# A two-layer attention and correlation network on one core: a planner's durations, the places it waits for, and when loads and token sums are queued

## The chip, the cores and the metric

The kernel runs on one core of a Trainium2 chip. The time is the device time of one execution in microseconds (us); three executions of the kernel before took 2810.83, 2817.05 and 2821.6 us, and the median, 2817.05, is the figure to which the change is compared. A separate, profiled execution took 2814.8 us, and all views below are of that one.

The engines named here: TensorE (PE in the profile; PEld is its weight load), VectorE (DVE), ScalarE (ACT), GpSimd (POOL) and SyncE (SP), whose queue issues nearly all DMAs.

## What is computed

Eight images of 768 channels and 32 x 32 = 1024 tokens pass two layers, each added to its input. All is f32.

```python
# layer 0
x_flat = gn(x) as tokens                       # 1024 x 768
q, k, v = x_flat @ W_qkv.T, 12 heads of 64
var_v, var_k = var(v, -1, ddof=1), var(k, -1, ddof=1)
attn = softmax(var_v @ var_k.T * scale)        # outer product of two vectors, per head
x = x + (attn @ v) @ W_proj.T + b_proj
# layer 1
f = gn(x)
n = f / max(norm(f over channels), 1e-12)
corr = [sum over channels of shifted(n) * n, for 28 shifts of a 7 x 7 window]
x = x + conv_w @ concat(f, corr) + conv_b
```

The scores of a head are an outer product of two vectors of 1024 numbers, so a block of exponentials needs only one row (broadcast to 128 partitions) and one column.

## The kernel before

*Products.* The large products are done by a seven-product scheme on 2 x 2 blocks (a form of Strassen's): a unit is one of the seven products p of one output group. Keys and values take 28 units of each half of the heads for an image (three matmuls of 384 columns each, two instructions a matmul); the projection and the convolution take 21 units each (three of 512 columns). Sums of weight blocks are made once at the start and kept in DRAM; sums of token blocks are made for each image, for keys and values by GpSimd (line 520, `make_sums`) and for the two wide products by VectorE (`TokenSums`, lines 931 to 967: `first` makes t1, `second` t2, `thirds` overwrites a part of f, `fourth` makes t4; three VectorE instructions each). Products p = 6 read t2, p = 7 the thirds, p = 4 t4.

*Weight blocks.* `KvStream` (line 267) keeps five buffers of 576 KB for key and value blocks, each of which serves two units; `TStream` (line 288) keeps seven of 192 KB for the wide products, one for each unit. After a unit's matmuls are queued, `done` (line 283) or `Wide.unit` (line 892, its last line) queues the refill of the freed buffer on SP at once.

*Attention.* The twelve heads are six pairs; pairs 0 to 2 need the first half of keys and values, 3 to 5 the second. A pair has eight steps t. A step makes two tiles of exponentials on ScalarE (line 651, from a broadcast row `bc` that a DMA reads back from DRAM, `vdr`), and four matmuls (line 676), two instructions each, add to one PSUM tile `av`. TensorE takes four steps in a row, a run of 32 instructions. There are six buffers of exponentials, three steps' worth (AHEAD). The denominators come in one of two ways: on ScalarE, by a second pass of exponentials with an accumulated sum (line 661, from the row `bk`, read back from `kdr`), or, for the pairs in SUMMED (3 to 5; in image 0 all but pair 1), by VectorE, which adds the tiles of exponentials into two `acc` tiles, two additions of 128 x 1024 a step; a buffer of such a pair is free when both its products and its addition are done. After the last step the pair's `av` is copied by ScalarE (`evacuate`, line 696), the sums are made into inverses, by way of DRAM (`di`, `den`, `rd`) or, for the last pair, from PSUM by VectorE, and `finish` multiplies.

*Second layer.* It runs one image behind: while image b has its attention, image b - 1 has its Gram products (line 974, eight of them) and its convolution (`Conv`, line 1063), whose residual, image b - 1 after layer 0, is read back from DRAM into the freed image buffer. `Corr` turns the Gram products into 28 correlations; matmuls of these with their weights join two convolution units at a time (line 905).

*The order.* Nothing is scheduled by the compiler. The program is emitted once, in Python, and an engine executes its instructions in the order in which they were emitted; the semaphores keep them right. That order is decided by a planner (`Clock`, line 71), which passes a planned time `now` on as units are queued on TensorE: `KV_US`, `T_US`, `CORR_US` and `STEP_US` are what it takes a unit, a joined correlation and a step to be, and 2.5 us for a Gram product. `later.after(us, job)` emits a job when the planned time has come that far. ScalarE has a planned time of its own, `act`: two rows of work wait for it, the exponentials (each 2 x EXP) and ScalarE's sums (each SUM); `feed_act` (line 92) emits the next when `act` is at most 1 us ahead of `now`, and of both rows takes the exponentials, unless these are ready over 0.3 us later. `clock.dve` is VectorE's planned time (line 126).

`exp_work` (line 835) says when a step's exponentials may be made: when the pair's rows are taken to be there (`rows_at`, line 644: 6 us after they are asked for) and fewer than AHEAD steps are made and not yet multiplied. `can_run` (line 865) lets a run of four steps begin when three steps are made and the last of them is due within 1 us. In `work_off` (line 1139) a run goes ahead of the remaining units, and while the attention is not over, units worth TAIL = 14 us are kept back for its end.

```python
841            def may():
842                if ("c", 1) not in pair.rows_at or self.made - self.done >= AHEAD or self.made - self.summed > LAG:
843                    return None
844                return max(pair.rows_at["c", 1], clock.now if self.made - self.done == AHEAD - 1 else 0.0)
...
875            return self.made >= self.done + AHEAD and self.exp_at <= clock.now + 1.0
```

After attention and convolution comes the projection (`project`, line 1156), four units of which need no more than pairs 0 to 2; the fifth waits for the last pair's result. Its residual, the image, is loaded into the buffer of f.

In image 0 there is no second layer to fill with, and the loads of the correlation weights (`load_corr_weights`, line 396, due at planned time 150), 29 of them with the copy to the second half of the partitions, fall into its attention.

Of the kernel before, what the change touches and what calls it, by code (L numbers as in the profile page):

```python
# [18 lines left out]
HP = NH // 2  # L19
MT = N // P  # L20
# [21 lines left out]
AHEAD, LAG = 3, 4  # L42
# [2 lines left out]
TBLOCKS = 7  # L45
HELD = 12
TAIL = 14.0
EXP, SUM, STEP_US = 1.08, 1.28, 1.92
KV_US, T_US, CORR_US = 1.95, 2.58, 0.9

# [99 lines left out]
def two_layers(ctx, tc, x, wkv, wproj, bproj, wconv, wcorr, bconv, out):  # L152
    nc = tc.nc
# [5 lines left out]
    xnpool = pool("xnpool", 1)  # L159
# [22 lines left out]
    clock = Clock()  # L182
    later = clock
# [16 lines left out]
    def image_tile(pl, tag, name):  # L200
        return pl.tile([P, J, N], F32, tag=tag, name=name)

    def load(t, src, *queues):
        for j in range(J):
            (queues or (nc.sync,))[j % max(len(queues), 1)].dma_start(out=t[:, j, :], in_=src[:, j, :])
        return t
# [60 lines left out]
    class KvStream:  # L267
# [13 lines left out]
                self.loaded += 1  # L281

        def done(self, key):
            self.gone.add(key)
            del self.tiles[key]
            self.fill()

    class TStream:
        def __init__(self):
# [61 lines left out]
    xn = load(image_tile(xnpool, "xn", "xn0"), xv[0], nc.sync, nc.scalar)  # L351
    sums0 = WeightSums(0, nc.sync, nc.scalar)
    kv_stream, t_stream = KvStream(), TStream()
# [4 lines left out]
    for base, sign in ((0, 1), (3, -1)):  # L358
        nc.gpsimd.affine_select(
            out=group, in_=group, compare_op=ALU.is_ge, fill=0.0, base=base,  # L360
# [262 lines left out]
    class Pair:  # L623
# [13 lines left out]
        def rows(self, kind, e):  # L637

            pl, of = (bcpool, self.kv.vdr) if kind == "c" else (bkpool, self.kv.kdr)
            h = self.heads()[e][1]  # L640
            bc = pl.tile([P, N], F32, tag=f"b{kind}", name=f"b{kind}{self.b}_{self.hp}_{e}")
            nc.sync.dma_start(out=bc, in_=windows(of[self.half][h : h + 1, :], (0, P), (1, N)))
            (self.bc if kind == "c" else self.bk).append(bc)
            self.rows_at[kind, e] = clock.now + 6.0

        def exponentials(self, t):

# [155 lines left out]
    class Attention:  # L803


        def __init__(self, b, kv, ots):
            self.b, self.kv = b, kv
            self.pairs = []
            for hp in range(HP):
                self.pairs.append(Pair(b, hp, kv, ots[hp], self.pairs[-1] if hp else None))  # L810
            self.made = self.done = self.summed = 0
            clock.poll = self.load_rows
            for pair in self.pairs:
                for t in range(MT):
                    self.exp_work(pair, t)
                for e in range(2):
                    for t in range(MT):
                        self.sum_work(pair, t, e)
# [16 lines left out]
        def exp_work(self, pair, t):  # L835
            def may():
                if ("c", 1) not in pair.rows_at or self.made - self.done >= AHEAD or self.made - self.summed > LAG:
                    return None
                return max(pair.rows_at["c", 1], clock.now if self.made - self.done == AHEAD - 1 else 0.0)

            def job():
                pair.exponentials(t)
                self.made += 1
                self.exp_at = clock.act

            clock.act_work(2 * EXP, may, job)
# [30 lines left out]
        def run(self):  # L877
            hp, t0 = divmod(self.done, MT)
            for t in range(t0, t0 + STEPS):
                while t not in self.pairs[hp].exs:  # L880
                    clock.pass_time(0.25)
                self.pairs[hp].products(t)
                self.done += 1
                clock.pass_time(STEP_US)


    class Wide:
# [4 lines left out]
        def unit(self, g, p):  # L892
            w = t_stream.take(self.kind, g, p)
            pairs = [(w[:, k, :], self.operand(p, k)) for k in range(JH)]
            taken = lambda ps: self.take(g, p, ps)
            more = self.more(g, p) if self.more else None
            if more is None:
                banks.product(g, p, T_US, HF, pairs, taken)
            else:
                self.held.append((*banks.begin(g, p, HF, pairs, stop=False), taken, *more))  # L900
                if len(self.held) == 2:
                    self.join()
            t_stream.fill()

        def join(self):

# [156 lines left out]
    class Conv:  # L1063
# [7 lines left out]

        def start(self):
            if self.acc is None:
                self.acc = load(image_tile(xnpool, "xn", f"x1_{self.b}"), x1_dram[self.b])
            if self.b == NB - 1:
                self.sums.third = [expool.tile([P, N], F32, tag="ex", name=f"t3_{k}")[:, :HF] for k in range(JH)]
            self.sums.second()
            self.wide = Wide(
                "c", f"c{self.b}", self.acc, bconv_sb, self.sums.operand, lambda i, hf: self.done(i, hf, "f"), self.more
            )  # L1080
            ready.add(("acc", self.b))
            later.after(4.0, self.thirds)

        def more(self, g, p):

# [51 lines left out]
    x1_dram = {}  # L1137
# [94 lines left out]
    for b in range(NB + 1):  # L1232
        rest, attention, ots = [], None, None
        if b < NB:

            ots = [v.rearrange("p t r d -> p (t r d)") for v in kv.vt]
            rest += kv.units(1)
            attention = Attention(b, kv, ots)
        if b:
            clock.wait(("f", b - 1), ready=ready)  # L1240
            f, acc = layer1[b - 1]
            corr = Corr(b - 1, f)
            conv = Conv(
                b - 1, f, None if b < NB else acc, (lambda b=b: next_image(b + 1)) if b + 1 < NB else lambda: None
            )
            grams = [(2.5, (), lambda t=t: corr.gram(t)) for t in range(MT)]
            first, start = (0.0, (), conv.sums.first), (0.0, (), conv.start)
            if b < NB:
                for n, gram in enumerate(grams):
                    rest.insert(3 * (n + 1) + n, gram)  # L1250
                rest.insert(len(rest) - 4, first)
                rest += [start] + conv.units()
            else:
                units, parts = conv.units(), conv.corr_units()
                rest += [first, start] + units[:2] + grams + units[2:17] + parts[:1] + units[17:19] + parts[1:] + units[19:]
        elif NB > 1:
            rest.insert(len(rest) - 1, (0.0, (), lambda: later.after(24.0, lambda: load_image(1))))
        work_off(rest, attention)
        if b == 0 and NB > 1:
            later.after(24.0, lambda: first_norm(1, images[1], 1.0))  # L1260
        if b < NB:
            project(b, ots)
            if b + 1 < NB:
                clock.wait(("xn", b + 1), ready=ready)
                kv = KeysValues(b + 1, images[b + 1])
                work_off(kv.units(0))
            else:
                clock.wait(("f", b), ready=ready)
# [36 lines left out]
```

## Time and profile before

| | us |
|---|---|
| median of three executions | 2817.05 |
| profiled execution | 2814.8 |
| its span, first to last instruction | 2812.8 |
| granted TensorE clock, share of full | 0.992 |
| one image of images 1 to 6, from pair 0's first run to the next one's (1083.36 to 1423.52) | 340.2 |
| exponentials, line 651: 768, mean 1.139 each | 833.5 busy |
| ScalarE's sums, line 661: 352, mean 1.144 each, and 0.187 to read the sum out | 402.6 and 66.0 busy |
| VectorE's sums `acc<-acc,ex`: 364, mean 1.216 each | 419.3 busy |
| attention products, line 676: 3072, mean 0.605 each | 735.2 busy |
| DMA engines, mean busy share of 16 | 50.8% |

The span is the time between the first and the last instruction; about 2 us of the execution lie outside it. A mean of one instruction counts from its own start to its own end; instructions of one engine overlap, so the distance from start to start is shorter: four exponentials in a row take 4.25 us. Matmuls are drawn with ends that are modelled, two of them at a time on different columns for line 676, and a busy TensorE can be one that waits within a group: a group is measured from its start to the start of what comes next.

### The profile page before, as it was taken

What the parts mean: (1) busy time and instruction counts of PE and PEld (TensorE: products, weight loads), DVE (VectorE), ACT (ScalarE), POOL (GpSimd) and SP (SyncE); (2) the same over time, 40 slices, a digit from 0 to 9 for tenths busy, and PEclk for the clock granted to TensorE, in tenths of its full rate; (3) what the DMA queues carried; (4) which work ended last, traced back from release to release, by engine and by line L of the source; (5) the groups of instructions that cost most, each with busy time, mean ns of one, the idle gap of its engine ahead of it and who ended that gap; (6) DMA issues with size and microseconds to landing.
All of it is one profiled execution on the core that took longest, in us unless ns stands there. A gap on an engine that the chain in (4) does not pass through costs nothing.

```text
span 2812.8 us, 28872 instructions
## 1 busy us (share of the span) xinstructions
PE 2737.1 (97%) x9070; PEld 1287.5 (46%) x9070; DVE 1627.1 (58%) x4086; ACT 1365.5 (49%) x1875; POOL 310.9 (11%) x350
## 2 busy tenths in 40 slices
PE   6988999999999999999999999999999999999999
PEld 3432455335553355534554345543455334553354
DVE  4778733776337753477534875258642676437753
ACT  1466039820597106970088701985019840298300
POOL 3500120002200022000310002100121001210000
PEclk9999999999999999999999999999999999999999
DMA  8573354545554555536456265453654626535323
GB/s 298 195 255 113 124 170 132 177 134 192 174 146 140 181 160 168 161 118 204 152 161 188 85 210 166 149 173 94 225 183 114 190 77 229 167 107 165 111 83 95
DMA packets 320923, 447.67 MB, mean 159 GB/s; under 512 B 59862, under 2 KB 242870, under 8 KB 320770
## 3 DMA queue, kind: packets, MB, share of 16 engines
q1 hardware_dynamic: 318962, 440.70, 50.0%
q10 hardware_dynamic: 1808, 5.11, 0.5%
q8 instruction: 73, 1.20, 0.2%
q14 instruction: 80, 0.66, 0.1%
HBM read 377.83 MB, written 65.81 MB: 158 GB/s over the span
## 4 chain that ended last, share of the span: by engine, by line
PE 82%; DMA 9%; ACT 4%; DVE 2%; SPq 2%; issue 1%; POOL 0%; DVEq 0%; ACTq 0%; POOLq 0%
PE x L338 32%; PE av L676 19%; PE y L338 14%; PE z L338 9%; PE gr L979 4%; ACT ex L651 4%; DMA bc<-vdr 1%; DMA kv<-kvs 1%; DMA vdr<-rsv 1%; DMA bk<-kdr 1%; DMA kdr<-rsk 1%; DMA wt<-tsc 1%; DVE acc L146 1%; DMA v<-rows 1%; DMA f<-in_x_dram 1%
## 5 line engine op out<-in xcount | busy, mean ns | idle before, releaser
L651 ACT ACTIVATE ex<-bc,nk 128x1024 f32<-128x1024 f32 x768 | 833.5, 1139 | 363.8 <-DMA bc<-vdr 243.4
L676 PE MATMUL av<-ex,v 128*64 128x512 f32 x3072 | 735.2, 605 | 29.1 <-ACT v L209 15.2
L676 PEld LDWEIGHTS av<-ex,v 128*64 128x64 f32 x3072 | 229.6, 138 | 512.6 <-issue 366.4
L146 DVE TENSOR_TENSOR acc<-acc,ex 128x1024 f32<-128x1024 f32 x364 | 419.3, 1216 | 2.2 <-ACT ex L651 2.2
L661 ACT ACTIVATE junk<-bk,vm 128x1024 bf16<-128x1024 f32 x352 | 402.6, 1144 | 31.0 <-DMA bk<-kdr 25.4
L209 ACT COPY kp<-x 128x384 f32<-128x384 f32 x32 | 15.2, 479 | 716.8 <-PE x L338 716.8
L338 PE MATMUL y<-kv,s 128*128 128x384 f32 x768 | 267.0, 488 | 2.7 <-DMA kv<-kvs 2.7
L338 PE MATMUL x<-kv,s 128*128 128x384 f32 x768 | 262.5, 490 | 3.8 <-DMA kv<-kvs 3.8
L338 PE MATMUL x<-kv,xn 128*128 128x384 f32 x768 | 262.0, 490 | 3.8 <-DVE xn L146 3.3
L338 PEld LDWEIGHTS x<-kv,s 128*128 128x128 f32 x768 | 145.4, 191 | 111.5 <-issue 13.8
L338 PEld LDWEIGHTS x<-kv,xn 128*128 128x128 f32 x768 | 145.4, 191 | 108.5 <-issue 10.4
L338 PEld LDWEIGHTS y<-kv,s 128*128 128x128 f32 x768 | 143.5, 190 | 96.5 <-POOL s L525 3.3
L146 DVE TENSOR_TENSOR v<-y,v 128x128 f32<-128x128 f32 x192 | 43.8, 283 | 197.7 <-PE y L338 197.7
L979 PE MATMUL gr<-f 128*128 128x227 f32 (+1 forms) x672 | 131.2, 345 | 0.0
L338 PE MATMUL x<-v,wt 128*128 128x512 f32 x288 | 130.1, 597 | 0.0
L338 PE MATMUL z<-kv,xn 128*128 128x384 f32 x384 | 129.2, 486 | 0.0
L979 PEld LDWEIGHTS gr<-f 128*128 128x128 f32 x672 | 121.3, 191 | 13.5 <-issue 1.5
L446 POOL TENSOR_TENSOR rstda<-vea,neghalf 128x1 f32<-128x1 f32 x8 | 4.8, 596 | 1046.1 <-DVE vea L146 1046.1
L525 POOL TENSOR_TENSOR s<-xn 128x384 f32<-128x384 f32 x64 | 67.4, 1057 | 465.7 <-PE x L338 362.8
L338 PE MATMUL x<-f,wt 128*128 128x512 f32 x252 | 117.2, 601 | 0.0
L146 DVE BATCH_NORM_STATS2 kbn<-x 128x6 f32<-128x64 f32 x384 | 56.4, 215 | 91.8 <-PE x L338 91.8
L146 DVE BATCH_NORM_STATS2 vbn<-v 128x6 f32<-128x64 f32 x768 | 108.4, 210 | 0.0
(163 smaller groups left out, 2856.4 us busy)
## 6 DMA issues: line engine op xcount, KB each, us to landing
kv<-kvs SPq DMA_DIRECT2D x128, 576.0 KB
kv<-in_wkv_dram SPq DMA_DIRECT2D x96, 576.0 KB
bc<-vdr SPq DMA_DIRECT2D x96, 512.0 KB
f<-in_x_dram SPq DMA_DIRECT2D x48, 512.0 KB
xn<-in_x_dram SPq DMA_DIRECT2D x45, 512.0 KB
bk<-kdr SPq DMA_DIRECT2D x44, 512.0 KB
x1d<-f SPq DMA_DIRECT2D x42, 512.0 KB
x<-x1d SPq DMA_DIRECT2D x42, 512.0 KB
```

The lines of the kernel that those rows point to most:

```text
L146: return getattr(self.engine, name)(*args, **kw)
L209: nc.scalar.copy(to, at)
L338: nc.tensor.matmul(t, lhsT=lhsT, rhs=rhs, start=p in FIRST and k == 0, stop=stop and k == len(pairs) - 1, skip_group_check=True,)
L446: nc.gpsimd.tensor_tensor(self.rstd, ve, neghalf[:, 0:1], ALU.pow)
L525: nc.gpsimd.tensor_tensor(self.sums[g][:, 0], a[g][2], a[g][3], ALU.add)
L651: nc.scalar.activation(ex, self.bc[e], AF.Exp, scale=self.kv.nk[self.half][:, h, t : t + 1])
L661: nc.scalar.activation(junk, self.bk[e], AF.Exp, scale=self.kv.m2[self.half][:, h, t : t + 1], accum_out=self.sums[:, e, t : t + 1],)
L676: nc.tensor.matmul(self.av[e * HD : (e + 1) * HD, hf, :], lhsT=self.vt[:, t, e, :], rhs=exs[e][:, hf * HF : (hf + 1) * HF], start=t == 0, ...
L979: nc.tensor.matmul(ps[:, :n], lhsT=f[:, j, t * P : (t + 1) * P], rhs=f[:, j, t * P : t * P + n], start=j == 0, stop=j == J - 1,)
```

## The change

It alters numbers and the time of emission. No instruction of an engine is added or taken away, apart from the residual's six loads being written out one by one as before they were in a loop.

- The planner's durations: EXP 1.08 to 1.07, SUM 1.28 to 1.15, STEP_US 1.92 to 1.77, KV_US 1.95 to 1.94, T_US 2.58 to 2.6, CORR_US 0.9 to 1.05; a Gram product 2.5 to 2.35, the last and narrower one to 1.45.
- A key and value block's buffer counts as free, and its refill is queued, KV_US + 0.3 after the unit; a wide block's refill T_US + 0.3 after its unit.
- The rows of pairs 0 and 3 are taken to be there 9 us after they are asked for.
- `may` now takes as the time from which a step's exponentials can be made the end of the products of the step whose buffers it takes over, and for VectorE's pairs also the end of its sums, less one exponential. This is noted in `free_at` as each step is queued.
- The residual's six chunks are loaded in the order 0, 1, 3, 4, 2, 5, at 0, 1, 2.5, 4, 12 and 14 us after the convolution's start; `second` goes 3.5 us after the start instead of at it, `thirds` (and `fourth` behind it) 7 instead of 4.

```diff
-EXP, SUM, STEP_US = 1.08, 1.28, 1.92
-KV_US, T_US, CORR_US = 1.95, 2.58, 0.9
+EXP, SUM, STEP_US = 1.07, 1.15, 1.77
+KV_US, T_US, CORR_US = 1.94, 2.6, 1.05
...
         def done(self, key):
-            self.gone.add(key)
             del self.tiles[key]
-            self.fill()
+
+            def free():
+                self.gone.add(key)
+                self.fill()
+
+            later.after(KV_US + 0.3, free)
...
-            self.rows_at[kind, e] = clock.now + 6.0
+            self.rows_at[kind, e] = clock.now + (9.0 if self.hp % (HP // 2) == 0 else 6.0)
...
             self.made = self.done = self.summed = 0
+            self.free_at = []
...
-                return max(pair.rows_at["c", 1], clock.now if self.made - self.done == AHEAD - 1 else 0.0)
+                free = self.free_at[self.made - AHEAD] if self.made >= AHEAD else 0.0
+                return max(pair.rows_at["c", 1], free)
...
-                self.pairs[hp].products(t)
+                pair = self.pairs[hp]
+                pair.products(t)
+                self.free_at.append(max(clock.now + STEP_US, clock.dve - EXP if pair.summed else 0.0))
                 self.done += 1
...
-            t_stream.fill()
+            later.after(T_US + 0.3, t_stream.fill)
...
             if self.acc is None:
-                self.acc = load(image_tile(xnpool, "xn", f"x1_{self.b}"), x1_dram[self.b])
+                self.acc = image_tile(xnpool, "xn", f"x1_{self.b}")
+                for n, us in ((0, 0.0), (1, 1.0), (3, 2.5), (4, 4.0), (2, 12.0), (5, 14.0)):
+                    later.after(us, lambda n=n: nc.sync.dma_start(out=self.acc[:, n, :], in_=x1_dram[self.b][:, n, :]))
...
-            self.sums.second()
+            later.after(3.5, self.sums.second)
...
-            later.after(4.0, self.thirds)
+            later.after(7.0, self.thirds)
...
-            grams = [(2.5, (), lambda t=t: corr.gram(t)) for t in range(MT)]
+            grams = [(2.35 if t < MT - 1 else 1.45, (), lambda t=t: corr.gram(t)) for t in range(MT)]
```

## The prediction

> **What bounds the kernel now.** I read the page first, then the waits of TensorE, its timeline through one whole image, the chain of waits through the same stretch, and last the queue of SyncE (SP).
>
> The page's first part, busy time by engine:
> ```profile
> PE 2737.1 (97%) x9070; PEld 1287.5 (46%) x9070; DVE 1627.1 (58%) x4086; ACT 1365.5 (49%) x1875; POOL 310.9 (11%) x350
> ```
> TensorE is busy nearly throughout, so no other engine can be worth much unless it makes TensorE stand. Who does that, in total us, times and longest:
> ```profile
> PE av L676 <- ACT v L209: 15.2, 5, 4.1
> PE pma L431 <- DVE mva L146: 14.1, 1, 14.1
> PE av L676 <- ACT ex L651: 12.8, 16, 4.4
> PE x L338 <- DVE t2o L146: 8.0, 3, 6.9
> ```
> Start and image 0 hold most of that. But a busy matmul may be a waiting one, so I go by start times. TensorE's timeline in image 4 (the fifth): start, duration, group, and in brackets idle time before it:
> ```profile
> 1423.52 5.37 PE L676 MATMUL av<-ex,v 128*64 128x512 f32 x24
> 1429.17 2.97 PE L676 MATMUL av<-ex,v 128*64 128x512 f32 x8 [0.29 <-ACT ex L651]
> ...
> 1540.32 7.24 PE L676 MATMUL av<-ex,v 128*64 128x512 f32 x24
> 1547.80 2.97 PE L676 MATMUL av<-ex,v 128*64 128x512 f32 x8 [0.24 <-ACT ex L651]
> 1550.70 0.28 PE L785 MATMUL it<-ident,inv 128*16 128x128 f32 x1
> ...
> 1554.54 7.09 PE L676 MATMUL av<-ex,v 128*64 128x512 f32 x32
> 1561.56 2.84 PE L338 MATMUL x<-f,wt 128*128 128x512 f32 x6
> ```
> An undisturbed run of four steps takes 7.02 from start to start (1554.54 to 1561.56). The run at 1540.32, the first of pair 3, takes 10.38: 3.36 lost. The one at 1423.52, the first of pair 0, takes 8.55 (the next product starts at 1432.07): 1.53 lost. Counted this way over images 1 to 7: pair 0's first run loses 1.90, 1.65, 1.73, 1.53, 1.56, 4.66, 4.78 (17.8 in all); pair 3's 2.99, 2.88, 3.50, 3.36, 3.29, 3.43, 2.06 (21.5); the last pair's two runs (14.04 undisturbed) 1.52, 1.33, 1.29, 1.24, 1.51, 2.89, 2.01 (11.8). Together 51. The rest of an image runs without gaps. Image 0, which has no second layer to fill with, loses some 47 more: 172.71 to 204.25 holds 72 products worth 15.8 in 31.55, the three pair borders after it lose about 17, t2o 8.7 at 273 to 292, and the runs at 110.56 and before 126.52 another 5.
>
> The chain of waits at pair 3 of the same image, start and duration:
> ```profile
> 1522.25 8.86 DMA v<-rows
> 1535.24 4.95 DMA bc<-vdr
> 1541.33 4.25 ACT ex L651 x4
> ```
> and SP's timeline there and in image 0:
> ```profile
> 170.81 0.33 SPq L789 DMA_DIRECT2D di<-ir  x1
> ...
> 182.58 0.46 SPq L498 DMA_DIRECT2D vdr<-rsv  x1
> 183.08 1.13 SPq L748 DMA_DIRECT2D rd<-di  x2
> ...
> 1516.92 4.02 SPq L205 DMA_DIRECT2D x<-x1d  x6
> ...
> 1532.53 0.53 SPq L498 DMA_DIRECT2D vdr<-rsv  x1
> 1534.86 2.02 SPq L642 DMA_DIRECT2D bc<-vdr  x4
> ```
> VectorE had the row for vdr ready at 1527.8 (its copy starts at 1527.55, 0.28); it left at 1532.53. In image 0, 29 small loads of the correlation weights sit between 171.2 and 182.5, ahead of vdr and rd. What SP itself waits for:
> ```profile
> SPq L279 <- PE x L338: 428.7, 104, 14.6
> SPq L302 <- PE x L338: 301.8, 123, 10.7
> ```
> These are refills of weight buffers, queued before the product that frees the buffer has run; everything behind them waits too.
>
> [...] 24 products drawn as 7.24 need 24 x 0.219 = 5.27. [...] so a refill that waits holds the queue; the 428.7 above is that. [...] the trace's mean is 1.216, its start-to-start 1.145 (9.16 for eight). [...]
>
> **The change part by part.** No product, exponential or byte is added: 384 attention steps and 224 + 336 weight blocks stay. All edits move instructions within their engines' orders, through a planner's clock.
>
> *Durations.* A step was planned at 1.92 and takes 1.755; it becomes 1.77. Two exponentials and two sums of ScalarE were 2 x 1.08 + 2 x 1.28 = 4.72, become 4.44, and take 4.50 in the trace (1457.00 to 1461.53, 1461.53 to 1466.03). A Gram product goes from 2.5 to 2.35, takes 2.29; a joined correlation from 0.9 to 1.05, takes 1.06. Engine against engine little moves, since both sides were planned 6 to 9% long: by this alone about nothing. ScalarE is now planned 1.3% short: over the 24 steps of pairs 0 to 2, 1.4 us, a bit more where sums follow sums (1.28 against 1.15). The bound is 0 to +2 an image; I take +1, 8 with small shifts elsewhere.
>
> *Rows at +9 instead of +6 for pairs 0 and 3.* The planner releases a run when the third step's exponentials are due within 1 us: 6 + 3 x 2.16 - 1 = 11.5 after the rows are asked for, now 9 + 6.42 - 1 = 14.4. TensorE takes one more product (1.94 or 2.6) first; there are 28 and 21 to draw on, so it costs nothing there. Lost today: 1.5 to 3.5, and 4.7 in images 6 and 7. Of pair 0's 17.8 I take 15 (3 stay in images 6 and 7, where 4.7 exceeds the 2.9). Of pair 3's 21.5 I take 20, since vdr also leaves earlier, as follows.
>
> *Weight refills later* (1.94 + 0.3 and 2.6 + 0.3 after their product's issue). 219 and 329 DMAs reach SP about when their buffer is free, so they are issued about when they are now, but other DMAs pass them. Cover: a kv block serves two products, four other blocks 15.5 us, landing in about 5; a wt block has six units, 15.5, landing in up to 9.1 (the chain at 2204.42). A further 2.9 still fits. If the cover were gone, each late block would cost its excess, 0 to 2; I take 0.
>
> *Residual loads and token sums.* Six loads of 512 KB leave at 0, 1, 2.5, 4, 12, 14 instead of as one 4.02 us burst on SP, in order of need; the three token sums (1.88 each for three) go 3.5 later. Passed by: spread's nine small operations (about 1.9), vdr, bc. t2 has ten us of products before its use, at t2 +3.5 + 1.9; thirds and fourth are needed five units later still. Cost 0 (bounds -1 to +2, VectorE waiting at the first residual chunk 1.84 as now). vdr gains up to 4.7; included above.
>
> *Places freed by sums.* In summed pairs the planner now has a place free when VectorE's sum ends. Its next run is due later by about a unit where VectorE lags, which fills TensorE where it waits in the last runs: 5 of 11.8. Evacuation of a pair's result is planned at 1.97 after the last product, and one exponential step fewer stands ahead of it: in image 0, where ScalarE did two steps (224.60 x2 among them) between the end of the products and the copies, 2.1 at up to three pair boundaries: 4 of 6.3. There too, the shorter plan puts the 29 loads (due at planned 150) some 3 us of work later: with even chance behind vdr and rd, 8.6 saved or none: 4.
>
> Sum: -15 - 20 - 5 - 8 + 8 = -40. From the profiled execution's own 2814.8 (span 2812.8) that is 2774.8; its run lies 2.25 under the median of 2817.05: 2777.
>
> **Rivals.**
> *The waits move on* (0.22). The later runs meet a ScalarE that has started its own chain later; pair 0's wait for its bk rows (2.80 before a sum at 1426.84) stands ahead of the fourth step all the same. For it: these gaps end in a DMA. Against: 2.9 us more cover is larger than most gaps. Then only a quarter of 51 goes: 2817 - 12 = 2805.
> *Image 0 gives its whole due* (0.10): 8.6 + 6.3 + 3 at 126.52, and last runs fully: another 20, 2757.
> *Attention ends too late* (0.18). VectorE's sums are planned at 1.215 each against 1.145, and every run of pairs 3 to 5 may be put off by a unit: 6 x 2.58 = 15.5, and 6 from the rows. Behind the last run lie 26.4 us of second-layer units (1608.65 to 1635.09); the planner keeps 14 back, so 12.4 can be spent. Beyond, TensorE waits: 21.5 - 12.4 = 9.1 in each of seven images, 64, less the 42 of first runs and image 0 that stay: 2839. It decides from about 18 us of delay an image. Against it: at a pair's border both planners wait for the same denominators, so only three runs move: about 8.
>
> **How the numbers follow.** 0.50 for the main case, 2760 to 2800. Measurement tells about 0.5%, 14 us: faster is under 2803. Faster: 0.50 + 0.10 + 0.06 of the first rival = 0.66. Same: 0.16 + 0.02 of the last = 0.18. Slower 0.16. Range 2752 to 2826: it takes in the first rival and the shallow part of the last, and leaves out some 0.04 below, 0.12 above.
>
> **What would show it.** Runs of pair 0 and 3 at 7.1 from start to start; L279 and L302 waits on SP cut to a third; vdr issued within a microsecond of its row; x<-x1d no longer in one piece; fewer than eight units behind the last run. Wrong would be: those runs whole, but new gaps at x<-t2o or at the last pair (the last rival), or kv and wt among what TensorE waits for.

## The result and the profile after

The changed kernel takes 2890.72 us (median of four executions, 2885.1 to 2893.15) against 2815.65 for the kernel before on the same chip. The ratio is 1.0263 [1.0237, 1.0289]: slower by 75 us, where 40 less had been forecast. The profiled execution took 2892.71, its span is 2891.0 (before 2812.8), its granted clock 0.980 (before 0.992). "Loss" means from here on, as in the prediction, the time from a group's start to the start of what follows, less that of an undisturbed group.

The page's first part hardly shows it:

```profile
PE 2749.9 (95%) x9070; PEld 1286.9 (45%) x9070; DVE 1644.4 (57%) x4086; ACT 1359.9 (47%) x1875; POOL 311.3 (11%) x350
```

The same number of instructions, 95% instead of 97% of a longer span. What TensorE waits for does show it (line, releaser; total us, times, longest):

```profile
PE x L917 <- DMA cs<-cs: 29.1, 7, 5.0
PE x L342 <- DMA wt<-tsp: 24.0, 6, 6.1
PE av L680 <- ACT ex L655: 19.9, 12, 8.4
...
PE ct L1033 <- DVE dn L146: 10.2, 7, 1.5
```

The first two are new. Each comes about once an image, and both are DMAs. TensorE's timeline of image 4 (start, duration, group, in brackets the idle time before it) has pair 0's first run, pair 3's, and the two waits:

```profile
1468.66 5.37 PE L680 MATMUL av<-ex,v 128*64 128x512 f32 x24
1475.04 2.97 PE L680 MATMUL av<-ex,v 128*64 128x512 f32 x8 [1.01 <-ACT ex L655]
1477.94 2.57 PE L987 MATMUL gr<-f 128*128 128x227 f32 x12
...
1587.66 1.12 PE L917 MATMUL y<-cs,wcorr_sb 64*128 64x512 f32 x2
1593.07 2.07 PE L917 MATMUL x<-cs,wcorr_sb 64*128 64x512 f32 x2 [4.29 <-DMA cs<-cs]
1595.07 8.97 PE L680 MATMUL av<-ex,v 128*64 128x512 f32 x32
1603.97 2.84 PE L342 MATMUL x<-f,wt 128*128 128x512 f32 x6
...
1701.65 2.74 PE L342 MATMUL x<-v,wt 128*128 128x512 f32 x6
1708.39 4.38 PE L342 MATMUL x<-v,wt 128*128 128x512 f32 x6 [4.00 <-DMA wt<-tsp]
1712.61 2.74 PE L342 MATMUL y<-v,wt 128*128 128x512 f32 x6
```

Pair 0's run loses 2.26 (9.28 from 1468.66 to 1477.94, less 7.02), more than the 1.53 of before. Pair 3's loses 1.88 instead of 3.36. Ahead of that run now stand the first joined correlations, which before came behind it, and wait for `cs`. The group after each wait is long too: six matmuls at 1708.39 take 4.22 to the next group, where such a group elsewhere takes 2.6. The clock by stretches around the wait for `cs` (us of the stretch, PE busy, granted clock, DMA share, GB/s):

```profile
1588.00:1592.00 4.00, 0.78 (x2) 1.00 1.05 292
1592.00:1595.00 3.00, 1.93 (x2) 0.51 0.89 221
1595.00:1604.00 9.00, 9.00 (x34) 0.78 0.16 60
1604.00:1611.00 7.00, 7.00 (x23) 1.00 0.22 58
```

Four idle microseconds are followed by a stretch at half clock, and most of it falls into the run. So a wait costs more than its length: 1.6 us more at 1708.39 (4.22 instead of 2.6, with a clock of 0.66 from 1708 to 1713), and 2.8 more at 1593.07 (0.9 in the two joined products, 1.9 in the run). Over the whole span the lower clock accounts for at most (1 - 0.980) x 2891.0 = 58 us, before for at most (1 - 0.992) x 2812.8 = 23; at most, because part of the half clock falls into the waits themselves (1592.1 to 1593.07 of the one for `cs`).

The chain of waits, start and duration, names what each waited for:

```profile
1582.58 10.45 DMA cs<-cs
...
1687.94 8.81 DMA out_dram<-x
...
1699.79 8.46 DMA wt<-tsp
```

and SP's timeline says why these were late:

```profile
1579.27 1.77 SPq L646 DMA_DIRECT2D bc<-vdr  x4
1581.09 1.45 SPq L1084 DMA_DIRECT2D x<-x1d  x2
1582.58 0.82 SPq L1066 DMA_DIRECT2D cs<-cs  x1
...
1688.41 0.52 SPq L306 DMA_DIRECT2D wt<-tsp  x1
1696.83 2.92 SPq L205 DMA_DIRECT2D xn<-in_x_dram  x6
1699.79 1.26 SPq L306 DMA_DIRECT2D wt<-tsp  x2
```

*cs.* Two chunks of the residual, 512 KB each, and the four `bc` stand right ahead of the copy of `cs`, and the copy takes 10.45 to land. Now TensorE is ready for it some 5.5 after the issue. In the kernel before it had 15.1 us, since pair 3's run and one more unit stood in between (SyncE's line and TensorE's):

```profile
1538.38 0.83 SPq L1058 DMA_DIRECT2D cs<-cs  x1
...
1553.49 0.69 PE L909 MATMUL x<-cs,wcorr_sb 64*128 64x512 f32 x1
```

*wt.* The six loads of the next image (`xn`) wait on SP until the stores of results (`out_dram<-x`) have left their buffer, 7.8 us, to 1696.83. The weight block whose buffer came free at 1688.44 is queued 2.9 of planned time later, and so behind them. It is issued 11.35 after its buffer was free, and lands after TensorE's need. The same place in the kernel before:

```profile
1641.73 2.87 SPq L302 DMA_DIRECT2D wt<-tsp  x2
1649.52 3.01 SPq L205 DMA_DIRECT2D xn<-in_x_dram  x6
```

There the block was freed at 1640.34, went out in front of the six loads, and was used at 1657.03.

Both kernels have the same matmuls, so the time from each group's start to the start of the next can be added up by kind and compared. Of the 78.2 us by which the span grew, the joined correlations make 43 (51.0 to 94.4), `x<-v,wt` 37 (125.0 to 161.9), the Gram groups with the small `ct` product behind them 13 (142.2 to 154.9) and `y<-t1f` 8 (62.6 to 70.9). Attention products take 12 less (749.1 to 737.5), the denominators' products 5 less, the key and value products 6 less. It comes evenly: image 0 is 6 us longer, each of images 1 to 6 is 10 to 14 longer (1468.66 to 1820.91 is 352.25, before 340.2), image 7 is as long as before.

What SP waits for (line, releaser; us, times, longest), against 428.7 and 301.8 before:

```profile
SPq L279 <- PE x L342: 295.8, 86, 10.7
SPq L306 <- PE x L342: 284.6, 104, 10.7
SPq L997 <- ACT win L209: 196.9, 41, 15.4
```

The waits at refills are shorter, but nowhere near the third that had been forecast. The store of a Gram product's window, which must wait for ScalarE's copy, holds the queue longer than before (143.1 there).

### The profile page after: what moved, and what is told of

Same layout as the page of the kernel before. It is cut to its first block, busy times and chain, and to the rows that moved or that the text cites. A ratio compares the mean times of both kernels' runs of the same rounds, so it can differ in the third digit from the quotient of the medians.

```text
span 2891.0 us, 28848 instructions
## 1 busy us (share of the span) xinstructions
PE 2749.9 (95%) x9070; PEld 1286.9 (45%) x9070; DVE 1644.4 (57%) x4086; ACT 1359.9 (47%) x1875; POOL 311.3 (11%) x350
## 4 chain that ended last, share of the span: by engine, by line
PE 77%; DMA 12%; DVE 5%; SPq 3%; issue 2%; ACT 1%; POOL 0%; DVEq 0%; ACTq 0%; POOLq 0%
PE x L342 28%; PE av L680 19%; PE y L342 13%; PE z L342 9%; PE gr L987 4%; DMA cs<-cs 3%; DMA wt<-tsp 2%; DMA bk<-kdr 1%; DMA out_dram<-x 1%; DVE acc L146 1%; DMA v<-rows 1%; DVE dn L146 1%; PE x L917 1%; SPq L205 1%; ACT ex L655 1%
## 5 line engine op out<-in xcount | busy, mean ns | idle before, releaser
L680 PE MATMUL av<-ex,v 128*64 128x512 f32 x3072 | 714.3, 606 | 21.9 <-ACT ex L655 19.9
L680 PEld LDWEIGHTS av<-ex,v 128*64 128x64 f32 x3072 | 220.2, 139 | 497.9 <-issue 405.0
L342 PE MATMUL x<-v,wt 128*128 128x512 f32 x288 | 143.1, 642 | 24.0 <-DMA wt<-tsp 24.0
L146 DVE COPY acc<-ex 128x1024 f32<-128x1024 f32 x52 | 35.9, 718 | 143.8 <-ACT junk L665 80.9
L342 PEld LDWEIGHTS x<-v,wt 128*128 128x128 f32 x288 | 57.0, 204 | 99.4 <-issue 84.3
```

The costliest lines, as they stand in the source:

```text
L146: return getattr(self.engine, name)(*args, **kw)
L342: nc.tensor.matmul(t, lhsT=lhsT, rhs=rhs, start=p in FIRST and k == 0, stop=stop and k == len(pairs) - 1, skip_group_check=True,)
L680: nc.tensor.matmul(self.av[e * HD : (e + 1) * HD, hf, :], lhsT=self.vt[:, t, e, :], rhs=exs[e][:, hf * HF : (hf + 1) * HF], start=t == 0, ...
```

## The experiments

All ratios are to the kernel before, measured beside each group of runs (its median there was 2812 to 2818).

### Undoing one part in the changed kernel

Refills of wide blocks queued at once again:

```diff
-            later.after(T_US + 0.3, t_stream.fill)
+            t_stream.fill()
```

> The changed kernel with the wide blocks' refill queued at once again, as before. Theory 1 (the refill's delay lets the next image's six loads, which wait for the stores of the one before, go ahead of the blocks that the projection needs next): TensorE's wait for wt<-tsp (24.0 us, 6 times, and about 1.8 us after each at half clock) goes, 30 to 37 us less, ratio to before 1.013 to 1.016. Rival (the stall is contention of the six loads with any block, whatever the order on the queue): the wait stays, less than 8 us gained, ratio 1.024 or more.

2882.62, 1.023 [1.0215, 1.0246]. The wait for `wt` falls from 24.0 to 9.1, that for `cs` rises from 29.1 to 41.9: in image 4 the copy of `cs` leaves 3.4 us ahead of the join instead of 5.1, with one more weight block in front of it. So 8 us are gained in all, where 30 to 37 had been expected.

Two chunks of the residual later:

```diff
-                for n, us in ((0, 0.0), (1, 1.0), (3, 2.5), (4, 4.0), (2, 12.0), (5, 14.0)):
+                for n, us in ((0, 0.0), (1, 1.0), (3, 2.5), (4, 4.0), (2, 34.0), (5, 36.0)):
```

> The changed kernel with the residual's chunks 2 and 5 loaded 34 and 36 us after the convolution's start instead of 12 and 14. Theory 1 (these two stand right ahead of cs<-cs and slow it to 10.45 us): cs<-cs lands about 3 us sooner, TensorE's wait for it falls from 29 us to under 8 and the half clock after it goes, 25 to 45 us less, ratio to before 1.010 to 1.018. Rival (the rows bc, four of 512 KB, are what it waits behind, or the correlations are late from further up): under 10 us gained, ratio 1.023 or more.

2864.91, 1.0169 [1.0152, 1.0185]: 26 us less, as expected, though the wait for `cs` falls to 13.3 and not under 8. The two loads ahead of the copy are over half of that wait; the four `bc` still stand ahead of it.

Rows of pairs 0 and 3 at +6 again:

```diff
-            self.rows_at[kind, e] = clock.now + (9.0 if self.hp % (HP // 2) == 0 else 6.0)
+            self.rows_at[kind, e] = clock.now + 6.0
```

> The changed kernel with the rows of pairs 0 and 3 taken to be there after 6 us again. Theory 1 (the later rows put pair 3's first run behind the first joined correlations instead of ahead of them, so that these come 8 us of products sooner and find cs<-cs not landed): the run is ahead of the join again, the wait for cs<-cs goes (29 us and some 20 of half clock), pair 3's first run loses some 2 to 3.5 us again in each of seven images: 20 to 40 us less, ratio 1.012 to 1.020. Rival (the order of run and join has another cause): the wait for cs<-cs stays, ratio 1.024 or more.

2901.18, 1.0292 [1.0274, 1.031]: 10 us more, where 20 to 40 less had been expected. The wait for `cs` is gone, since pair 3's run stands ahead of the join again; but `av<-ex` waits 42.3 instead of 19.9 and `ct` 24.3 instead of 10.2. The later rows cause the wait for `cs`, and still the kernel is better with them. One reason is pair 0: its first runs lose 43.0 in images 1 to 7 here and 15.1 in the changed kernel. Most of the 43 is the price of the later refill of key and value blocks: put alone into the kernel before, it raises the loss of the same runs from 17.8 to 44.9 (below). Rows at +9 cover the larger part of that.

### One part alone in the kernel before

| part, put alone into the kernel before | us | ratio | what TensorE waits for that it didn't |
|---|---|---|---|
| wide blocks' refill later | 2833.08 | 1.0051 [1.0031, 1.007] | `wt` 24.0, six times |
| rows of pairs 0, 3 at +9 | 2835.88 | 1.0068 [1.0052, 1.0084] | see below |
| residual's loads and sums later | 2827.28 | 1.0033 [1.002, 1.0046] | `av<-ex` 27.4 (12.8) |
| durations | 2844.58 | 1.0099 [1.0084, 1.0114] | `ptv` 18.8, `av<-ex` 22.4 |
| places freed | 2855.07 | 1.0137 [1.012, 1.0154] | `ptv` 27.5, `den` 20.9 |
| key and value refill later | 2849.32 | 1.0109 [1.0088, 1.0131] | `av<-ex` 37.1 |

The edits are those of the diff. The expectations, in the order of the table:

> The kernel before with the wide blocks' refill delayed alone. Theory 1: TensorE waits for wt in the projection of images 0 to 5, some 4 us and half clock after it each time: 20 to 40 us more, ratio 1.007 to 1.014. Rival (the delay hurts only together with the faster plan): same time within 0.3%.

> The kernel before with the rows of pairs 0 and 3 taken to be there 3 us later, alone. Theory 1 (the step on these rows was right by itself; what it moves ahead of pair 3's run is paid only with the rest of the change): first runs of pairs 0 and 3 lose under 1 us each instead of 39 in all, no wait for cs<-cs, 20 to 35 us less, ratio 0.988 to 0.993. Rival (the join comes ahead of the run here too): TensorE waits for cs<-cs in seven images, ratio 1.000 to 1.010.

> The kernel before with the residual's loads spread and the token sums later, alone. Theory 1 (the loads of chunks 2 and 5 and the fourth sum come right where the correlations are finished): cs<-cs takes 8 us or more from issue to landing, TensorE waits for it 2 to 5 us in seven images, 15 to 45 us more, ratio 1.005 to 1.016. Rival (here pair 3's run still stands ahead of the joins and hides it): no wait for cs<-cs, vdr leaves 3 us or more sooner, ratio 0.992 to 1.000.

> The kernel before with the planner's durations changed, alone. Theory 1 (they change little between engines, but TensorE's units are queued 6 to 8 us an image earlier against what waits for a DMA by a fixed number of us): waits for ct and ptv appear, about 2 us an image, and some for cs or wt; 10 to 30 us more, ratio 1.003 to 1.011. Rival (as predicted): within 0.3% of before.

> The kernel before with the places freed by the products' and VectorE's ends, alone. Theory 1 (as predicted: runs of pairs 3 to 5 and evacuations move): last pair's runs lose 5 us less in all and image 0 some 4, ratio 0.995 to 1.000. Rival (exponentials are queued behind sums more often, so that fourth steps are late): waits of av for ex above 20 us, ratio 1.003 to 1.010.

> The kernel before with only the refill of key and value blocks put off by 2.24 of planned time. By the prediction's step nothing: 2817, since a block serves two products and the rest of five buffers covers 15.5. By the reading of the runs so far (SP's order is a chain of deadlines, and each part alone makes it worse), 2825 to 2835, with a new wait for kv or wt.

No part is faster alone, and added up they come to 0.050, twice what the change costs. Only the durations came out about as their first reading had it. The wide blocks' refill brought its wait, but cost 16 us instead of 20 to 40. The rows and the residual's loads cost 19 and 9 us without the wait for `cs` that one of their readings named, and the places freed and the key and value refill cost more than either of their readings allowed. Three of them show how.

*Rows at +9* did in the runs what the prediction said: pair 0's first runs lose 1.9 in images 1 to 7 together instead of 17.8, pair 3's 0 instead of 21.5. And the kernel is 19 us slower. The 37 came back at other places (waits of TensorE in this kernel):

```profile
PE x L338 <- DVE x L146: 16.3, 7, 2.7
...
PE y L338 <- DMA wt<-tsp: 10.8, 6, 2.6
PE ct L1025 <- DVE dn L146: 10.2, 7, 1.5
```

None of the three is among the larger waits of the kernel before. By groups, `y<-f` takes 17 more, `x<-f` 7, the Gram products 13, `x<-v,wt` 12. VectorE, which frees the PSUM banks of these units, itself waits for the inverses: `rd<-di` holds it for 9.56 us at 1543.92, since it left SP behind the gathers of the correlations, at 1538.73. Before, TensorE stood in pair 3's run at about that time, and the chain had those microseconds to come up; that this is the reason fits the order, but no run tests it. The join comes ahead of pair 3's run here too, and in image 4 its products start 5.8 us after the copy of `cs` is issued (1549.62), without a wait: between the four `bc` and the copy no chunk of the residual is issued.

*Places freed.* The small product `ptv` waits in the middle of a run, in image 4 on TensorE and on VectorE:

```profile
1545.57 5.37 PE L676 MATMUL av<-ex,v 128*64 128x512 f32 x24
1555.60 0.41 PE L495 MATMUL ptv<-ident,vm 128*48 128x128 f32 x1 [4.66 <-DVE vm L146]
1555.94 3.37 PE L676 MATMUL av<-ex,v 128*64 128x512 f32 x8
```

```profile
1552.02 0.75 DVE L146 SCALAR_TENSOR_TENSOR x<-x,bconv_sb,x 128x512 f32<-128x512 f32 x1 [6.17 <-DMA x<-x1d]
```

`vm` is made ten instructions behind the one that waits for the residual's first chunk. The residual's load was issued late, behind `rd`, and in the kernel before at 1516.92:

```profile
1544.73 4.05 SPq L205 DMA_DIRECT2D x<-x1d  x6
```

What the runs ask for at other times puts it at another place in the queue. The loss sits in pair 2's second run (40.7 in images 1 to 7) and pair 3's (19.8), which lost 0.6 and nothing before. With the durations alone it sits in the same two runs (28.8 and 25.0). In both kernels pair 3's first runs lose 0.7 or less instead of 21.5, and the last pair's two runs nothing instead of 11.8: the gaps that were to be closed are closed, and new ones stand next to them.

*Key and value refill later.* Pair 0's first runs lose 44.9 in images 1 to 7 instead of 17.8. SP, ScalarE and TensorE at this run in image 4:

```profile
1430.28 0.37 SPq L279 DMA_DIRECT2D kv<-kvs  x1
1431.28 1.74 SPq L646 DMA_DIRECT2D bc<-vdr  x4
1433.11 0.63 SPq L502 DMA_DIRECT2D kdr<-rsk  x1
1440.45 0.32 SPq L993 DMA_DIRECT2D windowed<-win  x1
1440.83 0.43 SPq L279 DMA_DIRECT2D kv<-in_wkv_dram  x1
1441.64 0.79 SPq L646 DMA_DIRECT2D bk<-kdr  x2
```

```profile
1437.78 2.42 ACT L655 ACTIVATE ex<-bc,nk 128x1024 f32<-128x1024 f32 x2 [29.02 <-DMA bc<-vdr]
```

```profile
1450.60 4.60 PE L680 MATMUL av<-ex,v 128*64 128x512 f32 x8 [3.33 <-ACT ex L655]
1455.13 4.16 PE L342 MATMUL x<-kv,s 128*128 128x384 f32 x12
```

The `bc` rows and the first exponentials in the kernel before:

```profile
1412.94 1.75 SPq L642 DMA_DIRECT2D bc<-vdr  x4
...
1416.88 1.15 ACT L651 ACTIVATE ex<-bc,nk 128x1024 f32<-128x1024 f32 x1 [26.50 <-DMA bc<-vdr]
```

The later refill sends a key and value block of 576 KB 1.0 us ahead of the four `bc`; before, it left 3.8 ahead. The first exponentials, which wait for `bc`, start 6.5 us after its issue instead of 3.9. ScalarE's copy `win` stands behind the first of them, the `windowed` store waits for that copy, and `bk` stands behind the store: it leaves 8.5 us after `kdr` (before 6.8). ScalarE's first sum waits for `bk`, the fourth step's exponentials stand behind the sum, and TensorE's wait of 3.33 is followed by a lower clock (0.64 from 1450.5 to 1455): the run loses 6.21 instead of 1.53. In images 1 to 7 of the changed kernel, which has the later refill, the exponentials start 5.6 to 7.4 us after `bc`, in the kernel before 3.9 to 4.8.

### The loads on another queue

The residual's loads and the next image's, six each, are queued by GpSimd instead of SP, in the changed kernel and in the one before:

```diff
-                    later.after(us, lambda n=n: nc.sync.dma_start(out=self.acc[:, n, :], in_=x1_dram[self.b][:, n, :]))
+                    later.after(us, lambda n=n: nc.gpsimd.dma_start(out=self.acc[:, n, :], in_=x1_dram[self.b][:, n, :]))
...
-                images.append(load(image_tile(xnpool, "xn", f"xn{b}"), xv[b]))
+                images.append(load(image_tile(xnpool, "xn", f"xn{b}"), xv[b], nc.gpsimd))
```

> The changed kernel with two sets of six loads, the residual's and the next image's, queued by GpSimd instead of SP; all else as changed. Theory 1 (the stalls are places on SP's queue: what stands behind loads that wait for their buffer [...]): the wait for wt<-tsp falls from 24 us to under 6, the gathers and vdr leave sooner and the wait for cs<-cs falls from 29 to under 15, 35 to 60 us less, ratio to before 1.004 to 1.014. Rival (the stalls are bandwidth, the same bytes at the same time): ratio 1.022 or more.

> The kernel before with the same two sets of loads queued by GpSimd. Theory 1: vdr no longer leaves 4.7 us late, pair 3's first runs lose under 1 us each instead of 21.5 in all, 12 to 25 us less, ratio 0.991 to 0.996. Rival (the time gained there is taken by what is due next, or the reduction over partitions that GpSimd does for the maxima now waits behind its loads): ratio 0.998 to 1.006.

> The kernel before with these loads queued by GpSimd and the rows of pairs 0 and 3 taken to be there 3 us later. Theory 1 (the later rows were paid for by SP's queue: rd and vdr behind gathers and loads): the waits for rd in VectorE's queue (103 us with the later rows alone) fall under 50, no wait for cs or wt, first runs undisturbed, ratio 0.985 to 0.993. Rival (the join before pair 3's run is early by itself): waits at the joins stay, ratio 1.000 to 1.007.

2851.3, 1.0117 [1.0102, 1.0132] for the changed kernel: the wait for `wt` is gone, that for `cs` stays at 28.6. The kernel before gains nothing by it, as the rival had it: 2817.86, 1.0001 [0.999, 1.0011], though pair 3's first runs lose 15.4 instead of 21.5. With rows at +9 on top, 2827.85, 1.0037 [1.0021, 1.0053]: the rows still cost 10, and VectorE's waits for `rd`, expected to fall under 50, stay at 106. So the loads were not what kept `rd` late there.

Then rows at +6 in the first of these, to take away both waits:

> The changed kernel with the residual's and the next image's six loads queued by GpSimd (which alone took its time to 2851 and its wait for wt to nothing) and with the rows of pairs 0 and 3 back at +6 (which alone took its wait for cs to nothing but brought 42 us at av<-ex and 24 at ct). If the waits for wt and cs are costs of their own, each removable, both are gone and what remains is about the kernel before: 2851 less 28.6 of wait and some 11 of half clock, about 2812, ratio 0.998. If what is removed is only passed on to the next deadline of the attention, the wait for cs is replaced by waits at av<-ex and ct of the same size and the time stays at 2845 to 2865, ratio 1.010 to 1.017.

2920.73, 1.0377 [1.0356, 1.0397], which neither reading expected. Both waits are gone, and `ct` waits 91.7. GpSimd's timeline and TensorE's in image 4:

```profile
1580.44 0.74 POOL L1084 DMA_DIRECT2D x<-x1d  x1
1592.43 1.05 POOL L1022 TENSOR_TENSOR rn<-m,neghalf 128x4 f32<-128x4 f32 x1 [11.25 <-issue]
```

```profile
1594.38 0.44 PE L1033 MATMUL ct<-ident,dn 128*80 128x128 f32 x1 [12.91 <-DVE dn L146]
```

VectorE had `m`, which `rn` needs, ready at 1576.8. GpSimd's small product `rn` came 15.6 us later, next in the queue after a load, and 11.25 after the issue of that load had ended; what held it in between the profile doesn't name. So the run says nothing on its question. With the residual's loads back on SP (next section, rows at +6 too) `ct` waits 30.0 instead of 91.7: the loads on GpSimd's queue cost the rest, by a way that isn't shown.

### One cause after the other

So only the next image's six loads were moved to GpSimd, the residual's left on SP: alone, with the rows at +6, and with the two chunks at 34 and 36.

> The changed kernel with only the next image's six loads queued by GpSimd, the residual's left on SP. If these loads alone are why the block wt comes late, its wait of 24 goes, with some 1.7 of half clock behind each, and the time falls by 35 to 40, to about 2853, as with both sets of loads on GpSimd. If the gain of that run came from the residual's loads, it stays above 2880.

> The same with the rows of pairs 0 and 3 back at +6. If the waits for wt and cs are costs of their own, both are gone: 2853 less 28.6 and some 11 of half clock, about 2815, ratio 0.999. If a removed wait brings the next deadline forward, waits at av<-ex (some 42) and ct (some 24) take the place of the one for cs, as with +6 alone, and the time is 2855 to 2870, ratio 1.014 to 1.019.

> The same as the first, with rows at +9, and chunks 2 and 5 of the residual at 34 and 36. Alone, the move of these chunks took 26 off and left 13 of the wait for cs. If the two costs add, 2853 - 26 = 2827, ratio 1.003 to 1.006. If they draw on the same slack, 2840 to 2853.

2850.95, 1.0119 [1.0102, 1.0135]; 2866.16, 1.0168 [1.0152, 1.0183]; 2829.51, 1.0045 [1.0031, 1.0059]. The first: these loads alone account for the wait at `wt`, 40 us with the half clock. The second: +6 removes the wait for `cs` and brings `av<-ex` 41.8 and `ct` 30.0, as it did without the move. The time is the one expected for a wait that is passed on, but the larger part isn't passed on from `cs`: pair 0's first runs lose 42.7 here, mostly the price of the key and value refill, which the later rows had covered. The third: a wait of 1.0 to 1.6 is left of the one for `cs`:

```profile
1552.52 1.12 PE L917 MATMUL y<-cs,wcorr_sb 64*128 64x512 f32 x2
1555.22 1.14 PE L917 MATMUL x<-cs,wcorr_sb 64*128 64x512 f32 x2 [1.57 <-DMA cs<-cs]
```

`cs<-cs` is issued at 1547.47 there and used 7.75 later. The two mendings nearly add: 40, then 21, where the chunks alone had given 26.

Last, this mended version without the later refill of key and value blocks, and without the places freed:

> The mended version of the changed kernel (next image's loads by GpSimd, chunks 2 and 5 at 34 and 36; 2829.5) with the key and value refills queued at once again. If the later refill has a price of its own, the 31 us of the run alone come back: about 2799, ratio 0.993. If the price belongs to the order it was put into (there bk behind windowed<-win), 2820 to 2840, ratio 1.001 to 1.008.

> The same mended version with the places freed as in the kernel before (no free_at). With a price of its own, 38 us come back: about 2792, ratio 0.991. If the price belongs to the order, 2820 to 2845, ratio 1.001 to 1.010, with ptv and den waits no smaller than before.

2813.24, 0.9993 [0.9985, 1.0] (20 executions), and 2839.67, 1.0081 [1.0064, 1.0098]. The refill costs 16 us here (15 by the ratios), 31 alone in the kernel before; in pair 0's first runs the loss falls from 16.2 to 0.4 without it, the same 16. Here the rows are at +9 and cover the rest. The places freed cost 38 alone, and are worth 10 here.

So three undone causes take back the whole of the loss: 2890.7 - 39.8 (next image's loads in front of the wide blocks) - 21.4 (residual's chunks in front of `cs`) - 16.3 (key and value refill) = 2813.2. The terms are differences of one series of runs, so they add up by themselves, and in another order the shares would differ somewhat. What is left of the change, with both mendings, is as fast as the kernel before, not measurably faster: its attention products take 24 us less than before, and `y<-t1f` 13, the Gram products 13 and the joins 8 more. No version here is faster than the kernel before.

## Why the prediction was wrong

*The first runs: the worth of the step failed.* "TensorE takes one more product (1.94 or 2.6) first; there are 28 and 21 to draw on, so it costs nothing there." Alone, the rows took away 37 of the 39 in the first runs, about the 35 forecast, and the kernel was 19 us slower. What failed is "costs nothing". A product drawn forward is not neutral: it brings nearer what the later products wait for. In the kernel before, the join of the correlations came behind pair 3's first run, with `cs` asked for 15 us ahead. The one more product that goes ahead of the run is the second of a pair of convolution units, their join follows it at once, and `cs` has 5.5. The working counted the products in hand and didn't ask what each of them needs. In the changed kernel the first runs' loss fell by 13 (17.8 to 15.1 and 21.5 to 11.6), and the time at the joins rose by 43.

*Weight refills: failed, and by a source that was not counted.* "A further 2.9 still fits… I take 0." The cover was worked out from buffers: units between free and use, against a landing time. That sum is right only if the refill is issued when it is queued. The 2.9 put the block behind six loads that wait for stores, and it left 11.35 late. The key and value block it put right ahead of `bc`, so that here others were late by the refill: the exponentials (6.5 us after `bc` instead of 3.9), and `bk` behind them. The prediction had the facts ("a refill that waits holds the queue", "other DMAs pass them") and used them in one direction only: what the refill no longer holds up. What then holds up the refill, and what the refill meets at its new place, were not asked. 40 and 16 us. In image 4 SP's queue stood 7.8 us at `out_dram<-x`, and with it the six loads and the blocks behind them.

*Residual's loads: failed.* "Cost 0 (bounds -1 to +2)." The operations passed were counted to the last chunk's planned time of 14, but the copy of `cs` falls just behind the chunks at 12 and 14. 21 to 26 us in the changed kernel, with the rows; alone, without the rows, 9, and no wait for `cs`. The rows alone brought hardly a wait for `cs` either. The cost is that of two edits meeting, and the parts had been priced one by one.

*Durations.* "By this alone about nothing", then 8: it was 28 alone. The reason given, "both sides were planned 6 to 9% long", holds roughly for steps, Gram products and ScalarE's work, but not for the units, whose planned 1.95 and 2.58 hardly change (1.94 and 2.6). So the engines' plans did move against each other; that this is what costs the 28 isn't shown. In the changed kernel the durations were not tried apart.

*Places freed.* The last runs gained the whole of their 11.8 in images 1 to 7 (5 forecast). That isn't shown to be the work of the places freed: the 11.8 are gone with these alone, with the durations alone, and in the mended version without the places freed too. Image 0, from which the prediction expected 8 less, is 6 longer in the whole change.

*Pair 0.* 15.1 of 17.8 stayed, where 3 were expected to. The first rival had a reason for it: "pair 0's wait for its bk rows (2.80 before a sum at 1426.84) stands ahead of the fourth step all the same". But the later rows alone left 1.9, and the mended version without the later key and value refill 0.4. So the step on pair 0 was right by itself, and the refill undid it. The sign of "the waits move on" was right; its price (a quarter of the gain kept) was far off, because it let a moved wait cost no more than the removed one. The new ones cost more, in the changed kernel partly by half clock (0.992 to 0.980). The last rival, attention ending too late, did not occur: in image 4 four units instead of eight are left behind the last run, and TensorE doesn't wait there.

*The signs named.* "Kv and wt among what TensorE waits for" was named as the mark of an error, and `wt` is there. Residual loads in more than one piece and fewer units behind the last run came true. First runs at 7.1 did not (9.28 and 8.90), nor refill waits down to a third (295.8 and 284.6), nor `vdr` within a microsecond of its row (row at 1569.9, issue at 1573.87, 4.0 late; before 4.7).

Not settled: what the durations, the Gram products with their `ct` wait and `y<-t1f` (some 26 us that remain in the mended version) cost apart from the rest, and why the price of the places freed changes its sign between the two orders.

## What to carry to other kernels

When the bounding engine is 97% busy under a hand-made order, a gap that you close doesn't become gain until you have asked what is due next: go down the list of what is drawn forward, and for each find the DMA it needs and what stands ahead of that DMA (here a join that had 15 us for its copy, and then 5.5). A later queueing time is priced by what it falls behind in the queue, above all behind something that itself waits (here 40 us), and by what it falls in front of (here 16), not by the buffers in hand. Try edits of a planner singly and together: here six that cost 0.3 to 1.4% each when alone, less one of them and with two sets of loads moved, came to the time from which they started.

## What the runs showed of the hardware

In the changed kernel, waits of TensorE of 3 us and more cost more than their length. Between 320 and 2700 us, all 13 gaps of 3.09 us or more (by modelled ends) met 3.41 or 6.83 us of half clock, which began in the gap or within 0.6 us behind it; the nine gaps of 1.32 to 1.66 met none, and there is none between 1.66 and 3.09. Shorter gaps met it elsewhere: two of 2.35 and 1.97 in the kernel before, 3.41 us each, and in the changed kernel with both mendings the clock was 0.70 from 1555 to 1558, behind a wait of 1.57. What it costs: in the changed kernel, a group behind a wait of 4.00 took 4.22 instead of 2.6, a run behind a wait of 4.29 8.90 instead of 7.02.

The copy of `cs`, 240 KB, landed in 10.45 us behind two residual chunks and four `bc` while the DMA engines were fully busy (share 1.05 from 1588 to 1592). From its issue to the product that waits for it are 9.7 to 11.1 us in images 1 to 7 of the changed kernel, and 7.8 in images 1 and 4 of the version with both mendings, whose two chunks are loaded 22 us later.

Four broadcast rows of 512 KB were there for ScalarE 3.9 to 4.8 us after their issue in images 1 to 7 of the kernel before, where the last block of 576 KB had left 3.8 to 3.9 ahead of them, and 5.6 to 7.4 in the changed kernel, where it had left 0.7 to 1.0 ahead.
